# Causal-attention maxima over 64 queries of two heads instead of 128 queries of one, with the query stacks interleaved to match

## The chip, the cores and the metric

The kernel runs on one core of a Trainium2 chip. The metric is the device time of one execution in microseconds, from the first to the last instruction with the little that lies around them. Five engines work beside each other: TensorE (PE, with its weight loads PEld), VectorE (DVE), ScalarE (ACT), GpSimd (POOL) and SyncE (SP), which here only issues transfers.

## The reference

A pre-norm transformer layer on x of shape (4, 512, 1024), in float32: attention with 32 heads of 32, one shared key and value head (multi-query), ALiBi biases and a causal mask, and then a linear layer with 6-bit weights that are unpacked from int32.

```python
x = x + attn(layernorm(x), Wq, Wkv, Wo)
x = x + ffn(layernorm(x), qweight, weight_scale, weight_zero_point, bias)

def attn(hidden, Wq, Wkv, Wo):
    q = (hidden @ Wq).reshape(b, s, 32, 32)
    kv = hidden @ Wkv
    k, v = kv[..., :32], kv[..., 32:]
    scores = einsum('bqhd,bkd->bhqk', q, k) * 32 ** -0.5
    scores = where(causal, scores + slopes[:, None, None] * (pos_k - pos_q), -inf)
    attn = softmax(scores, axis=-1)
    return einsum('bhqk,bkd->bqhd', attn, v).reshape(b, s, h) @ Wo

def ffn(x, qweight, weight_scale, weight_zero_point, bias):
    w = (unpack_6_bit(qweight) - weight_zero_point) * weight_scale
    return einsum('bsk,nk->bsn', x, w) + bias
```

## The kernel before

Every float32 operand of a large matmul is split into a high part of few bits and the rest, both float32r, and the products hi*hi, hi*lo and lo*hi are summed in PSUM. `split` (lines 412 and 415) does this: ScalarE copies (`qh`, `aT`, `xT`, `xc`), VectorE subtracts (`ql` and the like).

Attention goes in 32 steps `i = b * 8 + g`, one for each batch element b and group g of four heads (`GH`). A step has three parts, which overlap with those of the steps around it:

- `queries` (products `pq`, L682): 24 products of 512 columns give the 128 rows of the group's queries (4 heads x 32) over 512 tokens in one PSUM buffer (`ps_q`, one). `qh` and `ql` go to HBM (`q_d`) and come back as a stack `qs` of 126 rows: 32 rows of qh, 32 of ql, 32 of qh again, 28 rows of biases (`qr_d`, prepared by the host), and two rows for the maxima. All these transfers have line 420. The stack has the layout (row, head, token); three are held.
- `maxima` (products `s`, L739): for each head and each tile t of 128 queries, the stack's 124 rows of these queries are the weights, and the keys `kst` up to the tile's end, 128(t+1) columns, stream past. The results go to PSUM buffers of 512 columns (`ps_s`, two), in banks that `S_BANKS` lists: 11 a step, 512 | 512 | 512 | 512 | 384 | 384 | 384 | 384 | 256+256 | 256+256 | 128 x 4. VectorE adds a causal mask and takes the maximum of each query over its keys (`junk`, L752). The maxima `mx` (128 x 16) are turned by TensorE (`trm`, L768), split (`mt0` by ScalarE, L774, and `mt1` by VectorE, L779), and written by two small transfers into the last two rows of the stack.
- `attention` (products `st`, L820): the keys are the weights and the stack streams, so that the scores come transposed (keys on partitions), with bias and minus the maximum already in. ScalarE takes the exponential (`p`, L830). For each of four key tiles GpSimd zeroes the upper triangle of the diagonal block of all four heads in one select (L839). TensorE multiplies by the values (`pav`, L849), GpSimd adds the four key tiles' p (L861), and TensorE sums them over the keys (`den`, L878). ScalarE copies pav to `a` (L867), which goes to `at_d` in HBM. `invert` takes the reciprocals of a batch element's denominators (L890).

After that come 16 token tiles: the output projection (`po`, L1048), the second layer norm, the linear layer (`pf`, L1168).

The order on each engine isn't written by hand. Every operation is recorded in `Work` with a cost, its inputs and its outputs; `order` then lists all of them by a model of the five engines and the transfers, several times forward and backward, and the instructions are issued in the order that came out. All ordinary transfers of the stacks go through one SP queue, in that order too. So a change in the cost or number of a few operations can move others on every engine.

Of the kernel before, what the change touches and what calls it, by code (L numbers as in the profile page):

```python
# [31 lines left out]
F32 = mybir.dt.float32  # L33
# [9 lines left out]
P = 128  # L43
NH = 32
HD = 32
GH = 4
S = 512
# [25 lines left out]
def bias_rows():  # L73
# [21 lines left out]
    qr = qr.reshape(NH // GH, GH, N_BIAS, S).transpose(0, 2, 1, 3)  # L95
# [246 lines left out]
def layer_kernel(  # L342
# [30 lines left out]
    for name, bufs in (  # L373
        ("const", 1), ("w", 2 * NG), ("xc", KC + 2), ("x", 4), ("qs", 3), ("q1", 1), ("p0", 2),
        ("pj", 1), ("stg", 3), ("kv", 2), ("small", 4), ("mt", 2),
    ):
        pool(name, bufs)
# [41 lines left out]
    def move(dst, src):  # L419
# [3 lines left out]
    qr_d = tc.dram_tile([NG, N_BIAS, GH, S], F32R, name="qr_d")  # L423
    at_d = tc.dram_tile([NG, P, B * S], F32, name="at_d")
    q_d = tc.dram_tile([4, 2, P, S], F32R, name="q_d")
# [16 lines left out]
    nc.gpsimd.affine_select(  # L442
        out=mask(),
        in_=mask(),
        pattern=[[-1, S]],
        compare_op=ALU.is_ge,
        fill=MASKED,
        base=S - P,
        channel_multiplier=1,
    )  # L450
# [14 lines left out]
    def prep_rows(at, g):  # L465
        dma(
            at, 229e3, lambda: nc.gpsimd.dma_start(out=qr_d[g], in_=q_rows[g]), [qr_i[g]], [],
            eng="POOL",
        )
# [205 lines left out]
    def queries(at, i):  # L675
# [15 lines left out]
        split(at, S, qh, ql, pq, qh, ql, pq)  # L691

        qs[i] = [(0, GH, new("qs", "qs", [P, GH, S], F32R, f"qs_{i}"))]
        for s, src in enumerate((qh, ql)):
            dma(
                at + 0.6 + 0.7 * s, 262e3,
                lambda s=s, src=src: move(q_d[i % 4, s], src()), [q_i[i % 4][s]], [src],
            )
        for h, n, q in qs[i]:
            dma(  # L700
                at + 1.0, 57e3 * n,
                lambda h=h, n=n, q=q: move(q()[R_BIAS:R_MAX, :, :], qr_d[g, :, h : h + n, :]),
                [(q, "b")], [qr_i[g]],
            )
            for r in range(3):
                dma(
                    at + 3.0 + 0.1 * r, 65e3 * n,
                    lambda r=r, h=h, n=n, q=q: move(
                        q()[ts(r, HD), :, :],
                        q_d[i % 4, r % 2, h * HD : (h + n) * HD].rearrange(  # L710
                            "(h d) q -> d h q", d=HD
                        ),
                    ),
                    [(q, r)], [q_i[i % 4][r % 2]],
                )

    def part(i, h):

        return next((q, h - first) for first, n, q in qs[i] if first <= h < first + n)


    S_BANKS = [((t, h),) for t in (3, 2) for h in range(GH)]
    S_BANKS += [tuple((1, h) for h in (2 * i, 2 * i + 1)) for i in range(2)]
    S_BANKS += [tuple((0, h) for h in range(GH))]
    ROWS = (0, 1, 2, "b")

    def maxima(at, i):
        b = i // NG
        k = kst[b % 2]
        mx = new("small", "mx", [P, GH * NT], F32, f"mx_{i}")  # L730
        for n, bank in enumerate(S_BANKS):
            ps = new("ps_s", "s", [P, S], F32, f"s_{i}_{n}")
            widths = [(t + 1) * P for t, _ in bank]
            places = [sum(widths[:m]) for m in range(len(bank))]

            def products(ps=ps, bank=bank, widths=widths, places=places):
                for (t, h), W, o in zip(bank, widths, places):
                    q, at = part(i, h)
                    nc.tensor.matmul(  # L739
                        ps()[:, o : o + W], q()[0:R_MAX, at, ts(t, P)], k()[0:R_MAX, :W],  # L740
                        start=True, stop=True,
                    )
            pe(
                at + 1.2 * n, widths, products, [ps],
                [(q, r) for q in {part(i, h)[0] for _, h in bank} for r in ROWS] + [k],
                more=sum(45.0 if w == P else 5.0 for w in widths),
            )
            for (t, h), W, o in zip(bank, widths, places):
                junk = new("q1", "junk", [P, S], F32, f"junk_{i}_{t}_{h}")
                dve(  # L750
                    at + 1.2 * n + 0.3, W,
                    lambda ps=ps, junk=junk, t=t, h=h, W=W, o=o: nc.vector.tensor_tensor_reduce(  # L752
                        out=junk()[:, :W],
                        in0=ps()[:, o : o + W],
                        in1=mask()[:, S - W :],
                        scale=1.0,
                        scalar=-3e38,
                        op0=ALU.add,
                        op1=ALU.max,
                        accum_out=mx()[:, h * NT + t : h * NT + t + 1],  # L760
                    ),
                    [(mx, (t, h))], [ps], more=125.0,
                )
        at += 1.2 * len(S_BANKS)
        N = GH * NT
        tr = new("ps_misc", "misc", [P, P], F32, f"trm_{i}")
        pe(
            at, [P], lambda: nc.tensor.transpose(tr()[0:N, :], mx(), ident()), [tr], [mx]  # L768
        )
        for s in range(2):  # L770
            m = new("mt", f"mt{s}", [N, P], F32R, f"mt{s}_{i}")
            if s == 0:
                hi = m
                act(at + 0.2, P, lambda: nc.scalar.copy(hi(), tr()[0:N, :]), [hi], [tr])  # L774
            else:
                lo = m
                dve(
                    at + 0.4, P,
                    lambda: nc.vector.tensor_tensor(  # L779
                        lo(), tr()[0:N, :], hi().bitcast(F32), ALU.subtract  # L780
# [3 lines left out]
            for h, n, q in qs[i]:  # L784
                dma(
                    at + 0.5 + 0.2 * s, 2e3 * n,
                    lambda m=m, s=s, h=h, n=n, q=q: move(
                        q()[R_MAX + s : R_MAX + s + 1, :, :], m()[h * NT : (h + n) * NT, :]
                    ),
                    [(q, f"m{s}")], [m],  # L790
                )
# [6 lines left out]
    def attention(at, i):  # L798
        b, g = divmod(i, NG)
        k = kst[b % 2]  # L800
# [5 lines left out]
        for n, (j, heads) in enumerate(ST_BANKS):  # L806
# [3 lines left out]
            runs = []  # L810
            for first, m, q in qs[i]:
                lo, hi = max(first, heads[0]), min(first + m, heads[-1] + 1)
                if lo < hi:
                    runs.append((
                        q, slice(lo - first, hi - first), slice(lo - heads[0], hi - heads[0])
                    ))

            def products(ps=ps, j=j, runs=runs):
                for q, mine, place in runs:
                    nc.tensor.matmul(  # L820
                        ps()[:, place, :], k()[0:R_ALL, ts(j, P)], q()[0:R_ALL, mine, j * P :],
                        start=True, stop=True,
                    )
            pe(
                at + 1.2 * n, [len(heads) * W / len(runs)] * len(runs), products, [ps],
                [q for q, _, _ in runs] + [k], more=5.0,
            )
# [8 lines left out]
            if done[j] == GH:  # L836
                def select(j=j):
                    d = pr[j]()[:, :, 0:P]
                    nc.gpsimd.affine_select(  # L839
                        out=d, in_=d, pattern=[[0, GH], [1, P]], compare_op=ALU.is_ge,  # L840
                        fill=0.0, base=0, channel_multiplier=-1,
                    )
                pool_op(at + 1.2 * n + 0.9, 650.0, select, [pr[j]], [pr[j]])
# [23 lines left out]
        act(at + 15.4, S, lambda: nc.scalar.copy(a(), pav()), [a], [pav])  # L867
# [433 lines left out]
```

## Time and profile before

| | |
|---|---|
| median of 3 runs | 828.51 us (828.41 to 833.47) |
| the profiled execution's own time | 830.86 us |
| its span, first to last instruction | 828.9 us |
| granted TensorE clock, mean | 0.993 |
| TensorE busy | 802.1 us |
| VectorE busy | 572.4 us |
| GpSimd busy | 515.7 us |
| ScalarE busy | 369.4 us |
| DMA share of the hardware queue | 57.4% of 16 engines |

"Busy" counts an instruction from its start to its end; TensorE's matmuls overlap, so its busy share is no measure of how much work it could still take. The chain of work that ended last is followed back from the last instruction: at each step to what released it. The first 535 us or so are attention, the rest the token tiles.

### The profile page before, as it was taken

To read this page: it belongs to the slowest core of one execution; us is meant where nothing else is said; L and a number is where in the kernel's file an instruction comes from. 1 tells how busy PE (TensorE), PEld (TensorE's weight loads), DVE (VectorE), ACT (ScalarE), POOL (GpSimd) and SP (SyncE) were. 2 spreads that over 40 slices of the span, in tenths; PEclk is the share of its full clock that TensorE was granted. 3 is DMA by queue.
4 is the path that set the end of the run, shared out by engine and by line. 5 is a ranking of instruction groups with operands and counts; after the bars stand their busy time and mean duration, and the time that the engine had idled before them with its cause. 6 is when DMAs were issued, how large, how long until landed. Compare 5 with 4: busy or idle time off the path is not lost.

```text
span 828.9 us, 13434 instructions
## 1 busy us (share of the span) xinstructions
PE 802.1 (97%) x4480; PEld 595.8 (72%) x4480; DVE 572.4 (69%) x1491; ACT 369.4 (45%) x659; POOL 515.7 (62%) x442
## 2 busy tenths in 40 slices
PE   5989999999999999999999999999999999999997
PEld 5766677776566767666766667667888888888885
DVE  7576876478676469866358656645988867678755
ACT  4336664545665354755365564340142323333320
POOL 4337968285968185876388997778556445554323
PEclk9989999999999999999999999999999999999999
DMA  7997662486742397463457774626975675565321
GB/s 221 245 249 214 186 173 63 123 221 216 207 112 82 91 257 227 116 162 113 153 138 220 200 215 141 232 51 165 254 169 137 138 184 127 137 164 131 102 51 51
DMA packets 131796, 133.39 MB, mean 161 GB/s; under 512 B 42964, under 2 KB 93140, under 8 KB 130704
## 3 DMA queue, kind: packets, MB, share of 16 engines
q1 hardware_dynamic: 130912, 129.01, 57.4%
q0 software_dynamic: 816, 3.53, 1.5%
q8 instruction: 35, 0.57, 0.3%
q14 instruction: 33, 0.27, 0.1%
HBM read 85.58 MB, written 39.85 MB: 151 GB/s over the span
## 4 chain that ended last, share of the span: by engine, by line
PE 87%; DMA 4%; DVE 4%; issue 2%; POOL 1%; ACT 1%; SPq 0%; DVEq 0%; ACTq 0%; POOLq 0%
PE po L1048 21%; PE pq L682 18%; PE pf L1168 13%; PE s L739 9%; PE st L820 9%; PE pav L849 8%; PE den L878 3%; PE pkv L616 2%; PE tr L598 2%; DVE junk L752 2%; POOL p L861 1%; DMA q_d<-ql 1%; DMA qs<-q_d 1%; ACT p L830 1%; DMA qs<-qr_d 1%
## 5 line engine op out<-in xcount | busy, mean ns | idle before, releaser
L752 DVE CUSTOM_DVE_ANT_0 junk<-s,mask 128x256 f32<-128x256 f32 (+3 forms) x512 | 250.4, 489 | 123.2 <-PE s L739 92.1
L861 POOL TENSOR_TENSOR p<-p,p 128x1536 f32<-128x1536 f32 (+2 forms) x96 | 230.4, 2400 | 20.2 <-PE pav L849 18.2
L830 ACT ACTIVATE p<-st 128x512 f32<-128x512 f32 (+1 forms) x352 | 184.0, 560 | 115.1 <-PE st L820 111.7
L682 PE MATMUL pq<-xc,wqh 128*128 128x512 f32 x512 | 195.8, 402 | 1.5 <-DVE ql L415 1.4
L1048 PE MATMUL po<-woh,aT 128*128 128x512 f32 x512 | 165.7, 390 | 0.0
L839 POOL TENSOR_SCALAR_AFFINE_SELECT p<-p 128x512 f32<-128x512 f32 x128 | 81.9, 645 | 104.4 <-ACT p L830 103.7
L739 PE MATMUL s<-kst,qs 124*128 124x256 f32 (+3 forms) x512 | 138.4, 339 | 7.0 <-DVE mx L752 3.3
L820 PE MATMUL st<-qs,kst 126*128 126x512 f32 (+1 forms) x352 | 125.6, 395 | 3.1 <-ACT p L830 2.6
L1168 PE MATMUL pf<-wf,xT 128*128 128x512 f32 x512 | 120.8, 390 | 0.7 <-DVE xT L415 0.7
L739 PEld LDWEIGHTS s<-kst,qs 124*128 124x128 f32 x512 | 89.0, 193 | 44.1 <-DVE mx L752 16.3
L682 PEld LDWEIGHTS pq<-xc,wqh 128*128 128x128 f32 x512 | 97.6, 191 | 21.6 <-DVE ql L415 2.1
L1048 PEld LDWEIGHTS po<-woh,aT 128*128 128x128 f32 x512 | 96.2, 188 | 21.4 <-ACT a L867 0.8
L1168 PEld LDWEIGHTS pf<-wf,xT 128*128 128x128 f32 x512 | 95.8, 188 | 21.5 <-DVE xT L415 1.7
L682 PE MATMUL pq<-xc,wql 128*128 128x512 f32 x256 | 101.6, 397 | 0.0
L1048 PE MATMUL po<-wol,aT 128*128 128x512 f32 x256 | 99.7, 390 | 0.0
L820 PEld LDWEIGHTS st<-qs,kst 126*128 126x128 f32 x352 | 65.0, 190 | 24.1 <-ACT p L830 9.7
L849 PE MATMUL pav<-p,kv 128*32 128x512 f32 (+3 forms) x1024 | 79.4, 436 | 0.4 <-POOL p L839 0.4
L849 PEld LDWEIGHTS pav<-p,kv 128*32 128x32 f32 x1024 | 29.9, 109 | 50.7 <-issue 38.0
L1188 POOL TENSOR_TENSOR x<-x,y 128x512 f32<-128x512 f32 x30 | 43.0, 1438 | 26.4 <-DVE y L1179 26.4
L1048 PEld LDWEIGHTS po<-wol,aT 128*128 128x128 f32 x256 | 48.1, 188 | 9.6
L1146 POOL TENSOR_TENSOR x<-x,rows 128x512 f32<-128x512 f32 x32 | 43.9, 1391 | 17.3 <-issue 10.1
L682 PEld LDWEIGHTS pq<-xc,wql 128*128 128x128 f32 x256 | 49.0, 191 | 5.8
(92 smaller groups left out, 850.5 us busy)
## 6 DMA issues: line engine op xcount, KB each, us to landing
qs<-q_d SPq DMA_DIRECT2D x96, 256.0 KB
x<-_attn_hidden_states_dram SPq DMA_DIRECT2D x31, 512.0 KB
q_d<-qh SPq DMA_DIRECT2D x32, 256.0 KB
q_d<-ql SPq DMA_DIRECT2D x32, 256.0 KB
at_d<-a SPq DMA_DIRECT2D x32, 256.0 KB
raw<-at_d SPq DMA_DIRECT2D x16, 512.0 KB
raw<-rden_d SPq DMA_DIRECT2D x64, 128.0 KB
out_dram<-x SPq DMA_DIRECT2D x32, 256.0 KB
```

Source lines behind the costliest of these rows:

```text
L682: nc.tensor.matmul(pq(), w()[:, c, :], xc[b, c]()[:, s, :], start=(c == 0 and n == 0), stop=(c == KC - 1 and n == 2),)
L739: nc.tensor.matmul(ps()[:, o : o + W], q()[0:R_MAX, at, ts(t, P)], k()[0:R_MAX, :W], start=True, stop=True,)
L752: lambda ps=ps, junk=junk, t=t, h=h, W=W, o=o: nc.vector.tensor_tensor_reduce(out=junk()[:, :W], in0=ps()[:, o : o + W], in1=mask()[:, S - ...
L820: nc.tensor.matmul(ps()[:, place, :], k()[0:R_ALL, ts(j, P)], q()[0:R_ALL, mine, j * P :], start=True, stop=True,)
L830: lambda ps=ps, own=own, j=j: nc.scalar.activation(pr[j]()[:, own, :], ps(), AF.Exp),
L839: nc.gpsimd.affine_select(out=d, in_=d, pattern=[[0, GH], [1, P]], compare_op=ALU.is_ge, fill=0.0, base=0, channel_multiplier=-1,)
L849: nc.tensor.matmul(pav()[ts(h, HD), j * P :], kv[b]()[:, j, HD:], pr[j]()[:, h, :], start=(j == 0), stop=(j == NT - 1), tile_position=(0, ...
L861: nc.gpsimd.tensor_tensor(d, d, pr[j](), ALU.add)
L1048: nc.tensor.matmul(po(), aT[s][1]()[:, c, :], w()[:, ts(n, HALF)], start=(c == 0 and m == 0), stop=(c == KC - 1 and m == 2),)
L1146: nc.gpsimd.tensor_tensor(d, d, rows["bias"][n][1](), ALU.add)
L1168: nc.tensor.matmul(pf(), xT()[:, s, c, :], wf[c]()[:, ts(n, HALF)], start=(c == 0 and s == 0), stop=(c == KC - 1 and s == 1),)
L1188: (nc.vector if last else nc.gpsimd).tensor_tensor(d, d, y(), ALU.add)
```

## The change

The maxima are taken for 64 queries of two heads at a time. With 64 queries a block ends at a multiple of 64, so the keys that stream past are 64, 128, ... 512 columns wide: 16 products a step as before, with 4,608 columns instead of 5,120. `S_BANKS` pairs them into nine banks of 512 columns: 512 | 512 | 448+64 (twice) | 384+128 (twice) | 320+192 (twice) | 256+256. For the 128 weight columns to have one step, the tokens of a tile are interleaved in the stacks: position 2m+o holds token 64o+m. So:

- `qh` and `ql` are written with a step of two words; `q_d` and the stack have the layout (row, tile, head, token), and the transfers between them move runs of 128 words (512 bytes) instead of 512 words; the host prepares the bias rows in that order.
- the weights of an `s` product are every second word of two heads' tile.
- the maxima are turned by two transposes of 8 columns each instead of one of 16, and `mt0` and `mt1` have 8 partitions of 256 elements instead of 16 of 128 (one buffer each instead of two).
- the causal select takes the two halves of a diagonal block one after the other, each 4 x 64 elements at a step of two.
- the copy to `a` and the reciprocals read at a step of two and put the tokens back in order.
- the model's extra cost of 45 ns for an `s` product of 128 columns is gone.

```diff
-    qr = qr.reshape(NH // GH, GH, N_BIAS, S).transpose(0, 2, 1, 3)
+    qr = qr.reshape(NH // GH, GH, N_BIAS, S // P, P // QB, QB).transpose(0, 2, 3, 1, 5, 4)
...
-        split(at, S, qh, ql, pq, qh, ql, pq)
+        def turns(t):
+            return lambda: t().rearrange("p (t m o) -> p t o m", t=NT, m=QB)
+        split(
+            at, S, turns(qh), turns(ql),
+            lambda: pq().rearrange("p (t o m) -> p t o m", t=NT, m=QB), qh, ql, pq,
+        )
+        q = qs[i] = new("qs", "qs", [P, NT, GH, P], F32R, f"qs_{i}")
...
-                lambda s=s, src=src: move(q_d[i % 4, s], src()), [q_i[i % 4][s]], [src],
+                lambda s=s, src=src: move(
+                    q_d[i % 4, s].rearrange("t p q -> p t q"),
+                    src().rearrange("p (t q) -> p t q", t=NT),
+                ),
...
+                lambda r=r: move(
+                    q()[ts(r, HD)].rearrange("d t h q -> d (t h) q"),
+                    q_d[i % 4, r % 2].rearrange("t (h d) q -> (t h) d q", d=HD).rearrange(
+                        "x d q -> d x q"
...
-    S_BANKS = [((t, h),) for t in (3, 2) for h in range(GH)]
-    S_BANKS += [tuple((1, h) for h in (2 * i, 2 * i + 1)) for i in range(2)]
-    S_BANKS += [tuple((0, h) for h in range(GH))]
+    NQ = S // QB
+    HP = GH // 2
+    S_BANKS = [((NQ - 1, u),) for u in range(HP)]
+    S_BANKS += [((NQ - 2 - m, u), (m, u)) for m in range(NQ // 2 - 1) for u in range(HP)]
+    S_BANKS += [tuple((NQ // 2 - 1, u) for u in range(HP))]
...
-            widths = [(t + 1) * P for t, _ in bank]
+            widths = [(e + 1) * QB for e, _ in bank]
...
-                for (t, h), W, o in zip(bank, widths, places):
-                    q, at = part(i, h)
+                for (e, u), W, at in zip(bank, widths, places):
+                    t, o = divmod(e, P // QB)
+                    rows = q()[0:R_MAX, t].rearrange("p h (m o) -> p o (h m)", m=QB)
                     nc.tensor.matmul(
-                        ps()[:, o : o + W], q()[0:R_MAX, at, ts(t, P)], k()[0:R_MAX, :W],
+                        ps()[:, at : at + W], rows[:, o, ts(u, P)], k()[0:R_MAX, :W],
                         start=True, stop=True,
                     )
...
-                more=sum(45.0 if w == P else 5.0 for w in widths),
...
-            at, [P], lambda: nc.tensor.transpose(tr()[0:N, :], mx(), ident()), [tr], [mx]
+            for o in range(P // QB):
+                nc.tensor.transpose(tr()[0:N, o, :], mx()[:, o, :], ident())
...
-                def select(j=j):
-                    d = pr[j]()[:, :, 0:P]
-                    nc.gpsimd.affine_select(
-                        out=d, in_=d, pattern=[[0, GH], [1, P]], compare_op=ALU.is_ge,
-                        fill=0.0, base=0, channel_multiplier=-1,
-                    )
-                pool_op(at + 1.2 * n + 0.9, 650.0, select, [pr[j]], [pr[j]])
+                for o in range(P // QB):
+                    def select(j=j, o=o):
+                        d = pr[j]()[:, :, 0:P].rearrange("p h (m o) -> p h m o", m=QB)[:, :, :, o]
+                        nc.gpsimd.affine_select(
+                            out=d, in_=d, pattern=[[0, GH], [1, QB]], compare_op=ALU.is_ge,
+                            fill=0.0, base=o * QB, channel_multiplier=-1,
+                        )
+                    pool_op(at + 1.2 * n + 0.9, 400.0, select, [pr[j]], [pr[j]])
...
-        act(at + 15.4, S, lambda: nc.scalar.copy(a(), pav()), [a], [pav])
+        act(
+            at + 15.4, S,
+            lambda: nc.scalar.copy(
+                a().rearrange("p (t o m) -> p t o m", t=NT, m=QB),
+                pav().rearrange("p (t m o) -> p t o m", t=NT, m=QB),
+            ),
+            [a], [pav],
+        )
```

## Prediction, made before the result was known

> **What bounds the kernel now.** I read first the busy times and the chain of work that ended last, then groups by shape, then single stretches.
>
> ```profile
> PE 802.1 (97%) x4480; PEld 595.8 (72%) x4480; DVE 572.4 (69%) x1491; ACT 369.4 (45%) x659; POOL 515.7 (62%) x442
> ...
> PE 87%; DMA 4%; DVE 4%; issue 2%; POOL 1%; ACT 1%; SPq 0%; DVEq 0%; ACTq 0%; POOLq 0%
> ```
>
> The chain runs through TensorE for 87% of 828.9 us. So a nanosecond taken from TensorE's own work counts in full, and one taken from another engine counts only where TensorE stands waiting for it. The places where it does are few. The chain of waits shows them:
>
> ```profile
> 32.50 7.62 DMA q_d<-ql
> 40.14 7.60 DMA qs<-q_d
> ...
> 443.45 3.47 POOL p L861
> ```
>
> At the start the second group's queries go out to HBM and come back as a stack, 7.6 us each way, with nothing else to do; near 443 us GpSimd's adds are late. The share by line adds 1.6% for `DVE junk L752`, that is 13.3 us of VectorE's maxima, scattered over the attention steps. Next, what one product of the maxima costs:
>
> ```profile
> 366.37 0.40 PE L739 MATMUL s<-kst,qs 124*128 124x256 f32 x2
> 366.61 0.39 PE L820 MATMUL st<-qs,kst 126*128 126x512 f32 x1
> ...
> 368.01 0.56 PE L739 MATMUL s<-kst,qs 124*128 124x128 f32 x4
> 368.41 0.62 PE L820 MATMUL st<-qs,kst 126*128 126x512 f32 x2
> ...
> 369.56 0.40 PE L739 MATMUL s<-kst,qs 124*128 124x512 f32 x1
> 369.79 0.34 PE L820 MATMUL st<-qs,kst 126*128 126x384 f32 x1
> 369.97 0.40 PE L682 MATMUL pq<-xc,wqh 128*128 128x512 f32 x1
> ```
>
> First number: start. The pitch (start to next start) is what counts, since durations overlap: 512 columns 0.23 us, 384 columns 0.18, 256 columns 0.24/2 = 0.12, 128 columns 0.40/4 = 0.10. From 512 to 256 the pitch falls with the columns; 128 would then cost 0.055 but takes 0.10. Narrow products have a floor.
>
> **The change, part by part** (32 steps, one for each group of four heads of a batch element).
>
> *Products of the maxima.* Before, 4 heads x widths 128, 256, 384, 512: 4 x (0.10 + 0.12 + 0.18 + 0.23) = 2.52 us a step. After, 2 pairs x widths 64 to 512 in steps of 64; between rows I interpolate: 0.11 for 192, 0.15 for 320, 0.205 for 448, and the floor for 64: 2 x (0.10 + 0.10 + 0.11 + 0.12 + 0.15 + 0.18 + 0.205 + 0.23) = 2.39. That is -0.13 x 32 = -4.2 us. Unknown: the 64-wide product, between 0.03 (columns alone, another -4.5 us) and 0.10; I take 0.10, the pitch of the nearest row, 128. Unknown too: the weights, which are now every second word of a stack row. No row has such a load. At worst each narrow product costs the duration of a load, 0.193 us (rival 1); a gain is excluded, since no load gets fewer words. I take no change.
>
> *One transpose more.* The maxima are turned by two matmuls instead of one:
>
> ```profile
> 329.83 0.11 PE trm L768
> ```
>
> 0.11 x 32 = +3.5 us, on TensorE. The copy to mt0 takes 256 elements for 128 (0.247 us; by ScalarE's 0.586 at 512, 0.36), the subtraction to mt1 0.423 (the row of kv<-trkv,part, 256 elements) for 0.273: together 0.26 us later for the two rows that end the stack. In the new order at least 4.2 us of TensorE work stands between trm and the first st product (4.1 before), so these are hidden; uncovered they would cost 0.26 x 32 = 8 us.
>
> *VectorE's maxima.*
>
> ```profile
> L752 DVE CUSTOM_DVE_ANT_0 junk<-s,mask 128x512 f32<-128x512 f32 x128 | 88.2, 689 | 51.2 <-PE s L739 42.6 <-DVE mx L752 0.5
> ...
> L752 DVE CUSTOM_DVE_ANT_0 junk<-s,mask 128x128 f32<-128x128 f32 x128 | 37.2, 291 | 9.8 <-PE s L739 3.3
> ```
>
> (689 - 291)/384 = 1.036 ns an element, plus 158 and an 83 ns read of the accumulator. The mean width falls from 320 to 288: 33 ns x 512 = 17 us less of VectorE. Only waits of TensorE give time back. I counted, in the order of both built programs with every matmul at its pitch, the places where a product needs one of the two PSUM buffers before VectorE can have read it: 18 places, 8.9 us before; 13 places, 3.1 us after (nine full banks a step instead of eleven). Against that trm now stands closer behind the last products (3.6 us in the mean, from 5.7): 1.4 us of new waiting. Sum -4.4; ends -13.3 (all of the chain's share) and 0.
>
> *The causal select by halves.*
>
> ```profile
> 1.07 0.29 POOL masks.py:199 TENSOR_SCALAR_AFFINE_SELECT ident<-ident 128x128 f32<-128x128 f32 x1
> ...
> 1.94 0.61 POOL L442 TENSOR_SCALAR_AFFINE_SELECT mask<-mask 128x512 f32<-128x512 f32 x1
> ```
>
> 0.83 ns an element and 0.18 fixed: 256 elements take 0.40. Two for one of 0.645 is +0.155, x 128 = +20 us of GpSimd. Mostly idle time takes it (GpSimd waits 104 us for p at that line), but not everywhere:
>
> ```profile
> 450.00:500.00 50.00, 48.94 (x301) 33.16 (x300) 33.35 (x124) 31.61 (x64) 48.03 (x35) 1.00 0.73 208
> ```
>
> The fifth engine number is GpSimd: 48.03 of 50 us busy. Some 3.3 steps of 0.62 us fall there: +2 us. Ends: 0, and 4 if 440 to 540 us is all tight.
>
> *Stacks in 512-byte pieces.* The five 256 KB moves of a step (qh and ql out, three in) have runs of 128 words instead of 512.
>
> ```profile
> 14.00:16.00 2.00, 1.91 (x10) 1.67 (x9) 1.42 (x3) 1.59 (x4) 0.00 (x0) 1.00 0.92 247
> 16.00:18.00 2.00, 2.00 (x10) 1.59 (x10) 2.00 (x4) 2.00 (x5) 0.00 (x0) 1.00 0.88 251
> 18.00:20.00 2.00, 2.00 (x10) 1.67 (x9) 2.00 (x5) 1.52 (x4) 0.98 (x1) 1.00 0.41 121
> 22.00:24.00 2.00, 2.00 (x11) 1.65 (x10) 1.89 (x2) 0.79 (x2) 1.48 (x2) 1.00 0.35 131
> ```
>
> The last two columns are the busy share of the DMA engines and GB/s. From 22 to 24 only qh moves, in 2 KB runs: 0.35 x 2 = 0.70 us for 262 KB. From 14 to 20 it is mostly Wq, in 512-byte runs: 2.21 x 2 = 4.42 us for 1,238 KB, 0.94 us for 262 KB. So +0.24 a move, +1.2 us of DMA a step. The issue costs the queue nothing more: raw<-at_d, 512-byte runs too, takes 0.43 us there, qs<-q_d 0.42. Outside full stretches it is hidden behind queries of later steps; if it is not, see rival 2. From 26 to 58 us the DMA share is about 1.0 and the chain goes through it; 3.5 steps are +4 us of DMA work, and the new order puts about 2 us less TensorE work before the second group's products. I take +3; ends 0 and 6. The Trainium skill, "DMA: Bandwidth & Descriptors", section "Why small descriptors are slow", gives a fixed cost of about three cycles a descriptor; estimated from it, 512-byte pieces cost (16 + 3) x 4 = 76 cycles for 67, 13%, and a step +0.46 us. The row says 34%, though of a load with other runs beside it; I go by the row.
>
> *Every second word elsewhere.* qh and ql are written at step two, a and the reciprocals read at step two. VectorE's nearest row is L920, 256 lone words at steps of three and four: 0.398 us median, no more than 0.423 for the 256 above. So ql stays at 0.687; the upper end is twice that, 22 us of VectorE, mostly in idle time. ql frees the one pq buffer: by the order, the next pq stands too close behind (under 1.5 us) for 1.8 us before and 3.2 after, +1.4; with ql at twice its time +5. The Trainium skill, "Vector Engine (DVE) Microarchitecture Reference", section 5.2, speaks against this part: a stream runs at full rate only in pairs of adjacent words, about 1.75 ns a column otherwise; estimated by it ql is 0.36 us longer and that term about 3 instead of 1.4. The row doesn't show the penalty.
>
> *Sum:* -4.2 + 3.5 - 4.4 + 2 + 3 + 1.4 = +1.3 us on the profiled execution, whose own time is 830.86 us (span 828.9, 1.96 around it). The median of the runs is 828.5, 2.35 lower; so 829.8 is forecast. The order differs in many places from the old one, which I allow +-8 us: 821 to 838 for this case. A measurement of this kernel tells about 1%, 8.3 us, from no change.
>
> **Rivals.**
> 1. *Slower: weights at step two load slowly.* Place: line 739, where narrow products follow each other. If the six of each pair up to 384 wide take 0.193, a step is 2 x (6 x 0.193 + 0.205 + 0.23) = 3.19 for 2.39, +25 us: 855. Banks now pair a wide with a narrow product, and often stand beside 0.23 us ones which cover a load, so half: 842. It decides from a pitch of about 0.15 (+9 us). For: no strided load in the trace. Against: the floor of 0.10 is already under the recorded 0.193, so loads have slack.
> 2. *Slower: the queries come back late.* Path of a step: qh 0.59, ql 0.69, issue 0.34, store 0.94, three loads 2.8, and about 2.6 us landing twice (k_rows, 60 KB, lands in 2.8): 10.9 us, 9.9 before. TensorE work between the last pq and the first s: at least 10.1 (six under 11.5), before 9.4 (three under 10.8). A queue of 3 us in front (two 512 KB moves) makes the shortfalls 25 us instead of 15: +10, so 840. For: stretches of share 1.0. Against: the chain meets this path only at the start.
> 3. *Faster: the waits for maxima all go,* and selects and moves are hidden: -4.2 + 3.5 - 13.3 + 1.4 = -12.6, so 816. For: nine even banks. Against: VectorE keeps 94% of its work here.
>
> **How the numbers follow.** Forecast 0.40, rival 1 0.15, rival 2 0.18, rival 3 0.27. Leaving a tenth out on either side: 813 to 846. The forecast's tails past 1% are small; faster 0.28, same 0.39, slower 0.33.
>
> **What would show it.** Right: pitch 0.10 at 64 and 128 columns, trm 0.11 twice, selects near 0.40, the junk group near 230 us busy for 250, its share of the chain near 1%. Wrong: a pitch over 0.15 at line 739 (rival 1); qs<-q_d in the chain after 100 us (rival 2); `DVE junk` nearly gone from the chain (rival 3); selects above 0.5, which would add 13 us and more to GpSimd's full stretch and the steps around it.

## The result, and the profile after

The changed kernel takes 840.82 us (median of 4 runs, 837.96 to 842.78); the kernel before, beside it, 829.46 (median of 4). The ratio is 1.0129, 95% interval 1.010 to 1.0157: slower by a little over one per cent. 829.8 was forecast, 813 to 846 as the range, 821 to 838 for the forecast's own case.

The profiled execution takes 841.85 us (span 840.1, 828.9 before; mean granted clock 0.988). From its page, first the busy times and the chain of work that ended last:

```profile
PE 799.9 (95%) x4512; PEld 598.7 (71%) x4512; DVE 552.5 (66%) x1491; ACT 374.0 (45%) x659; POOL 540.7 (64%) x571
...
PE 78%; DMA 8%; DVE 5%; POOL 3%; ACT 2%; issue 2%; SPq 1%; DVEq 0%; POOLq 0%; ACTq 0%
```

TensorE is busy 2.2 us less in a span 11.2 us longer, and VectorE 19.9 us less. The chain has lost nine points to other engines: DMA from 4 to 8%, GpSimd from 1 to 3%. From the same page the two groups whose price was forecast (busy, mean ns of one | idle before, and what ended it) and the hardware DMA queue (packets, MB, share of 16 engines), first before, then after:

```profile
q1 hardware_dynamic: 130912, 129.01, 57.4%
...
L752 DVE CUSTOM_DVE_ANT_0 junk<-s,mask 128x256 f32<-128x256 f32 (+3 forms) x512 | 250.4, 489 | 123.2 <-PE s L739 92.1
...
L839 POOL TENSOR_SCALAR_AFFINE_SELECT p<-p 128x512 f32<-128x512 f32 x128 | 81.9, 645 | 104.4 <-ACT p L830 103.7
```

```profile
q1 hardware_dynamic: 191328, 129.01, 61.4%
...
L762 DVE CUSTOM_DVE_ANT_0 junk<-s,mask 128x448 f32<-128x448 f32 (+7 forms) x512 | 233.5, 456 | 130.1 <-PE s L749 102.8
...
L847 POOL TENSOR_SCALAR_AFFINE_SELECT p<-p 128x256 f32<-128x256 f32 x256 | 106.3, 440 | 96.5 <-ACT p L837 95.7
```

The maxima take 233.5 us (about 230 forecast), a half select 0.440 us (0.40). The queue's time is 61.4% of 840.1 for 57.4% of 828.9: 40.0 us more on all 16 engines, over 160 moves of 256 KB 0.25 us each (0.24 forecast; the layout alone, in `pieces` below, gives 34.8 us, 0.22 each). Of the operations at step two only qh became slower, from 587 to 630 ns: ql takes 690 (687 before), the copy to a 587 (590), the reciprocals 919 (934). Estimated from the 1.75 ns a column of the Trainium skill, "Vector Engine (DVE) Microarchitecture Reference", section 5.2, ql would be some 0.36 us longer; these rows do not show it. mt0 takes 369 ns in the median and mt1 408 (0.36 and 0.423 forecast).

Next the products of the maxima. The timeline of TensorE (start, duration, what, how many) in the changed kernel, around 362 us:

```profile
362.05 0.40 PE L749 MATMUL s<-kst,qs 124*128 124x448 f32 x2
362.29 0.42 PE L829 MATMUL st<-qs,kst 126*128 126x384 f32 x1
362.55 0.40 PE L749 MATMUL s<-kst,qs 124*128 124x448 f32 x2
362.78 0.47 PE L686 MATMUL pq<-xc,wqh 128*128 128x512 f32 x1
363.10 0.40 PE L686 MATMUL pq<-xc,wql 128*128 128x512 f32 x1
363.33 0.39 PE L686 MATMUL pq<-xc,wqh 128*128 128x512 f32 x1
```

The two products 448 + 64 (named by the first form) take 0.24 us together, as if the 64 columns cost only their columns. But the product behind them takes 0.32 us to the next start (362.78 to 363.10), where the one after it takes 0.23 (363.10 to 363.33). The floor of a narrow product is there; it is paid at the next start. Over all such places from 100 to 550 us, the median of the following 512-column product is 0.31 behind 448 + 64, 0.28 behind 384 + 128, 0.25 behind 320 + 192 and 0.23 behind 256 + 256. So 64, 128 and 192 columns all cost about 0.11 us. (In the kernel before, the product behind four of 128 takes 0.29.)

**Where TensorE's time went.** From each product's start to the next one's, put down to the earlier, with recorded idle time put down to the product that waited, in the two profiled executions (us):

| | before | after | difference |
|---|---|---|---|
| s | 102.4 | 84.9 | -17.5 |
| trm | 2.0 | 9.5 | +7.5 |
| st | 90.1 | 95.4 | +5.3 |
| pq | 185.4 | 195.1 | +9.7 |
| po | 175.1 | 180.1 | +5.0 |
| pav and den | 105.1 | 105.6 | +0.5 |
| pf | 117.6 | 117.6 | 0.0 |

The maxima's products give 17.5 us. All of it and 10 more goes to others: part is the price of narrow products paid by the next one, part the second transpose, the rest waits and products at a lower clock. Two places stand out.

*The start.* The same timeline near 50 us, with the idle time before a product in brackets:

```profile
48.61 0.79 PE L686 MATMUL pq<-xc,wqh 128*128 128x512 f32 x1 [4.30 <-ACT wqh L491]
49.98 0.79 PE L686 MATMUL pq<-xc,wql 128*128 128x512 f32 x1 [0.57 <-POOL wql L493]
50.57 1.05 PE L686 MATMUL pq<-xc,wqh 128*128 128x512 f32 x2
51.42 0.63 PE L686 MATMUL pq<-xc,wql 128*128 128x512 f32 x1
```

and single stretches of it (busy time of PE, PEld, DVE, ACT, POOL; granted clock; busy share of the DMA engines; GB/s):

```profile
42.00:46.00 4.00, 1.01 (x4) 0.43 (x4) 3.74 (x12) 0.38 (x1) 1.18 (x1) 0.86 1.18 232
46.00:50.00 4.00, 0.82 (x2) 0.31 (x2) 1.02 (x5) 3.00 (x4) 2.34 (x4) 0.50 1.16 271
50.00:54.00 4.00, 4.00 (x10) 3.13 (x11) 0.00 (x0) 0.83 (x2) 1.66 (x2) 0.50 0.75 243
```

TensorE waits 4.3 us for a piece of Wq, whose transfer now stands behind the weights of the linear layer and the first stacks in SP's queue, while the DMA engines are full. The granted clock is 0.50 from about 45 to 55 us, so through most of the wait and some 6.5 us behind it, and a product of 512 columns takes 0.43 us instead of 0.23 (50.57 to 51.42 is two). The kernel before has such a stretch too, from about 53 us on, behind shorter waits. From 30 to 60 us TensorE is busy 21.83 us, before 25.67.

*The handover to the token tiles.* The last `st` starts at 555.59 us, before at 556.45: attention as a whole seems no slower. But before it 26 `pf` products had been done in the old order and 4 in the new one, and 16 `pav` products that stood before it now stand behind it: 22 x 0.23 + 1.6 = 6.7 us of work was left for later. The next tile's `po` waits for `raw` (the attention output times the reciprocals, on GpSimd), and `raw` for its transfers. From this tile on they use the buffers of p, so they can be issued only when `den` of the step before the last has read one, and `den` stands behind GpSimd's adds. The timeline of the kernel before (SPq is an issue):

```profile
543.43 1.29 POOL L861 TENSOR_TENSOR p<-p,p 128x512 f32<-128x512 f32 x1
...
546.18 0.38 SPq L1008 DMA_DIRECT2D raw<-at_d  x1
...
548.74 1.71 PE L849 MATMUL pav<-p,kv 128*32 128x512 f32 x16
550.38 6.23 PE L1168 MATMUL pf<-wf,xT 128*128 128x512 f32 x26
550.69 3.51 POOL L861 TENSOR_TENSOR p<-p,p 128x1536 f32<-128x1536 f32 x1
554.16 2.40 POOL L1025 TENSOR_TENSOR raw<-raw 128x1024 f32<-128x1024 f32 x1
556.45 0.40 PE L820 MATMUL st<-qs,kst 126*128 126x512 f32 x1
556.68 5.17 PE L1168 MATMUL pf<-wf,xT 128*128 128x512 f32 x22
...
561.69 0.39 PE L1048 MATMUL po<-woh,aT 128*128 128x512 f32 x1
```

and of the changed one:

```profile
544.90 3.76 POOL L869 TENSOR_TENSOR p<-p,p 128x1024 f32<-128x1024 f32 x2
...
551.02 0.38 SPq L1026 DMA_DIRECT2D raw<-at_d  x1
...
555.59 0.40 PE L829 MATMUL st<-qs,kst 126*128 126x512 f32 x1
555.92 1.71 PE L857 MATMUL pav<-p,kv 128*32 128x512 f32 x16
...
557.52 3.50 POOL L869 TENSOR_TENSOR p<-p,p 128x1536 f32<-128x1536 f32 x1
557.56 11.18 PE L1186 MATMUL pf<-wf,xT 128*128 128x512 f32 x48
560.97 2.40 POOL L1043 TENSOR_TENSOR raw<-raw 128x1024 f32<-128x1024 f32 x1
...
568.58 0.39 PE L1066 MATMUL po<-woh,aT 128*128 128x512 f32 x1
...
586.81 0.47 PE L1066 MATMUL po<-woh,aT 128*128 128x512 f32 x1 [2.82 <-DVE x L1076]
```

The adds of the step before the last end at 548.66 us for 544.72, the issue is 4.8 us later, the last step's long add stands ahead of `raw` in both, and `po` goes on 6.9 us later. TensorE does not stand idle for that: the work left over fills the time. It pays one tile later. The next tile's transfers can start only when `aT` has read the late `raw` (issue at 566.10, before 561.27), its `raw` ends at 577.4, and behind the additions that follow TensorE waits 2.82 us for `x`, before the `po` at 586.81; the kernel before has no recorded wait of `po`. The granted clock then falls to 0.50 for some 3.5 us, which makes the `po` products about 1.5 us slower in all.

From the start of the last `st` to the end of the last `po` it is 262.5 us, before 251.2. With the 6.7 us taken off, the token tiles lose 11.3 - 6.7 = 4.6 us, and attention, which left them that work, -0.9 + 6.7 = 5.8. Together 10.4, nearly all of the loss of this profile (11.0).

In the chain of waits (start, us, what), seven transfers of the stacks now stand between 60 and 560 us, 37.6 us together. In the kernel before there were two, 10.6 us together:

```profile
220.91 5.02 DMA qs<-mt
351.44 5.57 DMA qs<-qr_d
```

In the changed one these are among them:

```profile
101.88 5.46 DMA qs<-q_d
184.74 5.29 DMA qs<-qr_d
257.22 5.80 DMA qs<-qr_d
338.72 5.57 DMA qs<-mt
```

### The profile page after: what moved, and what is told of

Same layout as the page of the kernel before. It is cut to its first block, busy times and chain, and to the rows that moved or that the text cites. A ratio compares the mean times of both kernels' runs of the same rounds, so it can differ in the third digit from the quotient of the medians.

```text
span 840.1 us, 13606 instructions
## 1 busy us (share of the span) xinstructions
PE 799.9 (95%) x4512; PEld 598.7 (71%) x4512; DVE 552.5 (66%) x1491; ACT 374.0 (45%) x659; POOL 540.7 (64%) x571
## 3 DMA queue, kind: packets, MB, share of 16 engines
q1 hardware_dynamic: 191328, 129.01, 61.4%
## 4 chain that ended last, share of the span: by engine, by line
PE 78%; DMA 8%; DVE 5%; POOL 3%; ACT 2%; issue 2%; SPq 1%; DVEq 0%; POOLq 0%; ACTq 0%
PE po L1066 20%; PE pq L686 17%; PE pf L1186 12%; PE st L829 8%; PE s L749 7%; PE pav L857 7%; PE den L893 3%; DMA qs<-qr_d 3%; PE pkv L620 2%; PE tr L602 2%; DMA wo_st<-in_L_attn_Wo_dram 1%; POOL p L869 1%; DVE junk L762 1%; DMA qs<-mt 1%; ACT p L837 1%
## 5 line engine op out<-in xcount | busy, mean ns | idle before, releaser
L762 DVE CUSTOM_DVE_ANT_0 junk<-s,mask 128x448 f32<-128x448 f32 (+7 forms) x512 | 233.5, 456 | 130.1 <-PE s L749 102.8
L686 PE MATMUL pq<-xc,wqh 128*128 128x512 f32 x512 | 200.4, 408 | 6.2 <-ACT wqh L491 4.3
L847 POOL TENSOR_SCALAR_AFFINE_SELECT p<-p 128x256 f32<-128x256 f32 x256 | 106.3, 440 | 96.5 <-ACT p L837 95.7
L829 PE MATMUL st<-qs,kst 126*128 126x512 f32 (+1 forms) x352 | 129.0, 405 | 6.7 <-ACT p L837 4.1
L749 PE MATMUL s<-kst,qs 124*128 124x448 f32 (+7 forms) x512 | 116.9, 312 | 4.0 <-DMA qs<-qr_d 2.1
L749 PEld LDWEIGHTS s<-kst,qs 124*128 124x128 f32 x512 | 94.4, 198 | 29.5 <-issue 9.3
L1164 POOL TENSOR_TENSOR x<-x,rows 128x512 f32<-128x512 f32 x32 | 46.6, 1472 | 11.1 <-DVE x L1087 6.4
```

The lines of the kernel that those rows point to most:

```text
L686: nc.tensor.matmul(pq(), w()[:, c, :], xc[b, c]()[:, s, :], start=(c == 0 and n == 0), stop=(c == KC - 1 and n == 2),)
L749: nc.tensor.matmul(ps()[:, at : at + W], rows[:, o, ts(u, P)], k()[0:R_MAX, :W], start=True, stop=True,)
L762: nc.vector.tensor_tensor_reduce(out=junk()[:, :W], in0=ps()[:, place : place + W], in1=mask()[:, S - W :], scale=1.0, scalar=-3e38, op0=A ...
L829: nc.tensor.matmul(ps().rearrange("p h (t q) -> p h t q", q=P), k()[0:R_ALL, ts(j, P)], q()[0:R_ALL, j:, own].rearrange("p t h q -> p h t q"),
L847: nc.gpsimd.affine_select(out=d, in_=d, pattern=[[0, GH], [1, QB]], compare_op=ALU.is_ge, fill=0.0, base=o * QB, channel_multiplier=-1,)
L1164: nc.gpsimd.tensor_tensor(d, d, rows["bias"][n][1](), ALU.add)
```

## The experiments

Three theories were on trial. D: the moves in 512-byte runs bring queries and stacks back late. P: the second select holds GpSimd up. O: the planner's new order of the same work, not any price, makes the loss. Every experiment was timed against the kernel before on its own chip (medians 827.8 to 828.4 us).

**The 512-byte layout alone** (`pieces`): the kernel before with the order (row, tile, head, token) in the stacks and in HBM. The order on every engine stays that of before.

```diff
-    q_d = tc.dram_tile([4, 2, P, S], F32R, name="q_d")
+    q_d = tc.dram_tile([4, 2, NT, P, P], F32R, name="q_d")
-        qs[i] = [(0, GH, new("qs", "qs", [P, GH, S], F32R, f"qs_{i}"))]
+        qs[i] = [(0, GH, new("qs", "qs", [P, NT, GH, P], F32R, f"qs_{i}"))]
```

> The kernel before, with only the layout of the stacks and of the queries in HBM changed to (row, tile, head, token), so that the five 256 KB moves of a step go in runs of 512 bytes; tokens are not interleaved, the products, the selects and the order on every engine are those of before. Theory D (the 512-byte moves bring the queries back late, and this is most of what the change loses): 836 us or more, with waits for the stack in the chain after 100 us. Theory O (the new order loses most, and its own prices little): the moves cost what they cost at the start, +2 to +5 us, 831 to 834. Theory P (the second select on GpSimd): no change, 829.

835.34 us, ratio 1.009 (1.0065 to 1.0115): 7 us, between what D (836 or more) and O (831 to 834) expected. Its chain, by engine:

```profile
PE 85%; DMA 6%; DVE 3%; ACT 2%; issue 1%; POOL 1%; SPq 1%; DVEq 0%; ACTq 0%; POOLq 0%
```

DMA goes from 4 to 6%, with nothing else changed. So D has a price of its own, over twice the 3 us of the forecast. In this profile the last `st` is 4.0 us later than before and the stretch from there to the end of `po` is 251.2 us, to the tenth that of before: the price falls in attention alone, spread over it (TensorE busy 438.55 us from 100 to 550 us, before 442.17), not at the start, where the forecast had put it. How the longer moves reach TensorE is shown only in part: its recorded waits for stacks rise from 1.7 to 2.8 us, those for the maxima by 0.7, those for the exponentials by 0.5, and 2.0 us more have no releaser in the profile.

**The second select alone** (`selects2`): each select of before as two halves inside one recorded operation, again in before's order.

```diff
-                    d = pr[j]()[:, :, 0:P]
-                    nc.gpsimd.affine_select(
-                        out=d, in_=d, pattern=[[0, GH], [1, P]], compare_op=ALU.is_ge,
+                    for o in range(2):
+                        d = pr[j]()[:, :, ts(o, P // 2)]
+                        nc.gpsimd.affine_select(
+                            out=d, in_=d, pattern=[[0, GH], [1, P // 2]], compare_op=ALU.is_ge,
```

> The kernel before, with each causal select done as two, of the two halves of the diagonal block, in the same place of the same order (the model of the planner is told of one operation of 650 ns). Some 0.2 us more of GpSimd for each of 128 blocks, +24 us busy. Theory P: +6 us or more, 835. Theories D and O: 0 to +3 us, since GpSimd idles over 100 us in front of this line; 829 to 832.

832.52 us, ratio 1.006 (1.003 to 1.0089): 4 us, for 19 us more of GpSimd (534.6 busy; the halves are of adjacent words here and take 429 ns each, 440 in the changed kernel). That lies between P (835) and the others (829 to 832). P too has a price, twice the 2 us of the forecast, but a loosely known one: the ten runs go from 828.69 to 838.34. Where it falls is not shown, since the profiled run is the fastest of the ten, with a span 2.1 us under that of before's profile; in it GpSimd's share of the chain goes from 1 to 3%:

```profile
PE 89%; DVE 3%; POOL 3%; issue 1%; ACT 1%; DMA 1%; SPq 0%; DVEq 0%; ACTq 0%; POOLq 0%
```

**Both together** (`both`), still in before's order:

> The kernel before, with the 512-byte layout of the stacks and with each causal select as two halves in one recorded operation; the order on every engine is that of before. Alone the two cost 7 and 4 us. If they are prices of their own (theories D and P together, each on its own stretch of the chain): 10 to 12 us over before, ratio 1.013, which is the whole of the change's loss, so that the order would have nothing left to explain except what the cheaper products gave back. If they lean on the same slack (a stack that comes late gives GpSimd time): 7 to 8 us, 1.009.

836.44 us, ratio 1.0106 (1.0086 to 1.0126): 8.2 us, less than 7 + 4. The two may lean partly on the same slack, but the interval reaches from the one expectation to the other. Its chain:

```profile
PE 78%; DMA 8%; DVE 4%; POOL 4%; issue 3%; ACT 2%; SPq 1%; DVEq 0%; POOLq 0%; ACTq 0%
```

It is nearly the chain of the changed kernel. But the place differs: here the last `st` is 8.5 us late and the token tiles again take their 251.2; in the changed kernel, where TensorE has cheaper products, attention loses 5.8 us and the tiles 4.6.

**The same work in other orders** (`shaken`, `shaken2`): the kernel before, instruction for instruction, with one figure of the planner's model changed.

```diff
-                more=sum(45.0 if w == P else 5.0 for w in widths),
+                more=0.0,
```

> The kernel before with the same instructions in another order: the planner's model is not told of the 45 ns extra for a product of 128 columns (as in the changed kernel). It measures what an order alone moves. Theory O: a difference of 5 us or more, of either sign, with the same busy times; D and P: under 3 us.

```diff
-DMA_RATE = 280.0
+DMA_RATE = 270.0
```

> The kernel before with the same instructions in a second other order: the planner's model has a DMA rate of 270 instead of 280. Theory O: 833 to 842, like the first shaken one (836.9), which would make the order of before a good one among its like; if it is within 3 us of 828.4, an order moves less than that run said.

836.86 us, ratio 1.0094 (1.0065 to 1.0123), and 833.65, ratio 1.0063 (1.0043 to 1.0083). An order alone moves this kernel by 5 to 8 us, and both of these moved it up: of the three orders tried the one that the kernel before has is the fastest. In the first, the stretch from the last `st` to the end of `po` is 257.5 us instead of 251.2, with 4.2 us of recorded waits of `po` for `x`: the same place, and the same wait, as in the changed kernel, without any of its moves or selects.

**The planner told of the prices** (`told`): the changed kernel, in which the model counts the 256 KB moves and the selects as they are.

```diff
-                at + 0.6 + 0.7 * s, 262e3,
+                at + 0.6 + 0.7 * s, 350e3,
...
-                at + 3.0 + 0.1 * r, 262e3,
+                at + 3.0 + 0.1 * r, 350e3,
...
-                    pool_op(at + 1.2 * n + 0.9, 400.0, select, [pr[j]], [pr[j]])
+                    pool_op(at + 1.2 * n + 0.9, 430.0, select, [pr[j]], [pr[j]])
```

> The changed kernel, with the planner's model told that a 256 KB move in 512-byte runs costs 350 instead of 262 (in its units of kB) and a half select 430 ns instead of 400. The same instructions in another order. Theory D: the planner now leaves room for the moves, 828 to 836 instead of 841. Theory O: it lands anywhere from 828 to 845, and the waits sit in other places. Theory P: no change, 839 to 842.

830.84 us, ratio 1.0033 (1.0019 to 1.0047): the same work, the same moves, 8 us less than the changed kernel by the two ratios (10 by the medians, which are of different chips) and 0.3% over before. The timeline at the handover:

```profile
547.16 0.38 SPq L1026 DMA_DIRECT2D raw<-at_d  x1
...
554.67 2.40 POOL L1043 TENSOR_TENSOR raw<-raw 128x1024 f32<-128x1024 f32 x1 [0.51 <-DMA raw<-rden_d]
557.03 3.51 POOL L869 TENSOR_TENSOR p<-p,p 128x1536 f32<-128x1536 f32 x1
...
565.22 0.39 PE L1066 MATMUL po<-woh,aT 128*128 128x512 f32 x1
```

The transfers are issued 3.9 us earlier than in the changed kernel, and `raw` is now ahead of the long add: it waits 0.51 us for its own transfer and for nothing else. The wait of `po` for `x` is 0.2 us instead of 2.8, and the 4.3 us wait for Wq at the start is gone from the waits. Of the 9.1 us between the two spans, with work left over counted where it belongs, 3.4 come back in attention, 4.3 at the handover and 1.5 at the end. So most of the loss can be given back without touching a move or a select, which refutes P as the whole cause. The time fits D's expectation (828 to 836) as well as O's; but a later order, `unturn270` below, is told of the moves' price too and takes 838.5, so being told is not what does it.

**One select for the two halves** (`one_select`: the changed kernel; `told_one`: the kernel told of the prices). The pattern walks half by half inside each pair of positions, so its innermost run is 2.

```diff
-                for o in range(P // QB):
-                    def select(j=j, o=o):
-                        d = pr[j]()[:, :, 0:P].rearrange("p h (m o) -> p h m o", m=QB)[:, :, :, o]
...
+                def select(j=j):
+                    d = pr[j]()[:, :, 0:P].rearrange("p h (m o) -> p h m o", m=QB)
...
+                        out=d, in_=d, pattern=[[0, GH], [1, QB], [QB, P // QB]],
```

> The changed kernel with one causal select for each diagonal block and nothing told. Theory P: 840.8 - 5 = 836. Theory D: the moves keep it above 836, waits for the stack stay in the chain. Theory O: the order is new again, 828 to 845, without connection to GpSimd's busy time.

> The changed kernel with the planner told of the moves' cost (350 for 262) and with one causal select for each diagonal block, of 512 contiguous elements, whose pattern holds the interleave (64 m + 2 o steps in one instruction). 24 us less of GpSimd. Theory P (the second select is worth the 0.6% that it cost at the old order): 826 us, 4 to 6 below the 830.8 of the run that was only told. Theory O (orders differ by 1%): anywhere from 822 to 838. Theory D: 830.

971.38 us, ratio 1.1733 (1.1709 to 1.1757), and 971.05, ratio 1.1729 (1.1708 to 1.1749): a miss. The group in `one_select`:

```profile
L846 POOL TENSOR_SCALAR_AFFINE_SELECT p<-p 128x512 f32<-128x512 f32 x128 | 298.4, 2344 | 59.1 <-ACT p L837 59.1
```

2.34 us for 512 elements, where runs of 128 take 0.645. GpSimd becomes the bound, and the two orders come out alike. On theory P this tells only that enough GpSimd time is fatal.

**The linear layer's weights a step later** (`late`, on top of `told_one`):

```diff
-        unpack(T0 + (1.6 + 2.0 * (c % 3) + NG * (c // 3)) * STEP, c)
+        unpack(T0 + (2.6 + 2.0 * (c % 3) + NG * (c // 3)) * STEP, c)
```

> As the kernel that was told and has one select, and the unpacking of the first weight block (a 384 KB load, a transpose and a 512 KB store) starts one step of 15 us later, so that the stretch from 26 to 60 us with full DMA engines holds less. Theory D: the start gains back the 4 to 6 us of TensorE that the changed kernel lost from 30 to 100 us: 820 to 826. Theory O: no connection; 822 to 838.

981.28 us, ratio 1.1852 (1.1827 to 1.1877). With GpSimd as the bound it says nothing of the start; it was tried again below on a sound base.

**The halves put back by the exponential** (`unturn`): the kernel told of the prices, in which ScalarE's exponential reads its scores at a step of two and writes p in token order. The select is again one instruction in runs of 128, and the copy to a and the reciprocals are plain.

```diff
-                    pr[j]()[:, own, :], ps(), AF.Exp
+                    pr[j]()[:, own, :].rearrange("p h (t o m) -> p (h t) o m", o=P // QB, m=QB),
+                    ps().rearrange("p h (t m o) -> p (h t) o m", o=P // QB, m=QB), AF.Exp,
```

> The changed kernel with the planner told of the moves' price (350e3 for 262e3), in which the exponential reads its PSUM buffer at a step of two and writes p in token order: the causal select is again one instruction of 4 x 128 in runs of 128, and the copy to a and the reciprocals are plain. Theory P: the selects go back from 106 to 82 us, and about 4 us of the chain come back against the 830.8 us of the kernel that only tells the planner: 826 to 828, ratio 0.997 to 1.000. If the exponentials at step two cost (their mean of 512 columns over 0.62 us), ScalarE is later by the excess x 288. Theory O: a new order moves it by up to 6 us either way whatever the selects do.

830.79 us, ratio 1.0027 (1.0016 to 1.0039). From its page, the chain and the groups of the exponential and the select:

```profile
PE 90%; DVE 4%; issue 2%; ACT 1%; DMA 1%; POOL 0%; SPq 0%; DVEq 0%; ACTq 0%
...
L837 ACT ACTIVATE p<-st 128x512 f32<-128x512 f32 (+1 forms) x352 | 183.8, 559 | 118.7 <-PE st L829 111.6
...
L847 POOL TENSOR_SCALAR_AFFINE_SELECT p<-p 128x512 f32<-128x512 f32 x128 | 81.5, 643 | 117.0 <-ACT p L837 116.6
```

The step of two costs the exponential nothing (559 ns with and without), and the selects are back at 81.5 us. GpSimd has left the chain, from 6% in `told` to nothing; DMA went from 6 to 1%. The chain of `told`:

```profile
PE 80%; POOL 6%; DMA 6%; DVE 3%; issue 2%; ACT 2%; SPq 1%; POOLq 0%; DVEq 0%
```

The time stayed. The 826 to 828 us of theory P is missed: the 4 us of the second select that before's order had shown are not to be had here, or the new order took them. A chain share is not a price; what left the chain was replaced by waits for VectorE (`s` behind the maxima 5.2 us, in `told` 3.2) and by TensorE itself.

**The same with the later unpacking** (`unturn_late`: the edit of `late`) **and in another order** (`unturn270`: the edit of `shaken2`):

> The same, with the unpacking of the feed-forward weights recorded one step (15 us) later, so that its reads and writes of HBM leave the stretch from 26 to 58 us, in which the transfers are full. Theory D (the start is lost to the transfers' extra 0.25 us each): TensorE's busy time from 30 to 60 us rises from the 22.7 us of the told kernel to 24.5 or more, and the time falls by 2 to 4 us against the same kernel with the early unpacking: 823 to 826. If not the load of the transfers but the round trip of the first two groups' queries holds the start: no change there, and the time within 2 us.

> The kernel with the exponential in token order, the planner's DMA rate 270 for 280: the same instructions in another order. Theory O: 2 to 8 us from the same kernel at 280, either way, as two other orders of the kernel before were 5.5 and 8 us from it. If the order matters little in the changed kernel (nine even banks lean less on it): within 2 us.

`unturn_late`: 830.31 us, ratio 1.0037 (1.0018 to 1.0056). TensorE's busy time from 30 to 60 us rises from 24.13 us in `unturn` to 25.30; the 22.7 that the expectation started from is of `told`. The time expected, 2 to 4 us less, did not come: the medians differ by 0.5 us. The profiled execution, the fastest of its runs, shows where: its last `st` starts 5.1 us earlier than in `unturn`, but from 550 to 600 us TensorE is busy 47.65 us instead of 50.00, with a 2.3 us wait of `po` for `x`, and its span is only 1.8 us shorter. So a late start alone does not set the end.

`unturn270`: 838.5 us, ratio 1.0119 (1.0101 to 1.0137): 8 us from its twin by an order alone, so the changed kernel leans on its order as much as the kernel before.

No version beat the kernel before. The best of the changed ones stand 0.3 to 0.4% above it.

## Why the prediction was right and wrong

The time fell in the range, but 3 us past the forecast's own case. Slower by over 1% had been given 0.33, the forecast's side 0.39: the likeliest case did not come, and no single rival did either. That the range held is owed to its width and not to the sum, which said +1.3 us where 11 came; that rival 2 named 840 is luck, as shown below. Term by term, forecast against what the runs show:

- *Products, -4.2: right.* Own pitches after: 2 x 0.23 + 6 x 0.235 + 0.24 = 2.11 us a step, and 2 x (0.08 + 0.05 + 0.025) = 0.31 at the next starts, 2.42; before 2.52 and 0.06, 2.58. That is -0.16 x 32 = -5.1. The floor of 0.10 was the right guess, though it is paid one product later. Rival 1 is refuted: the loads at step two take 198 ns in the mean, 193 before, and no place shows a pitch that they could have made.
- *VectorE's waits, -5.8: the sign was right, the size is open.* Of the 17.5 us that `s` gave, (2.52 - 2.11) x 32 = 13.1 is own pitch, which leaves 4.4 for waits. Recorded are 2.8 (6.7 before, 3.9 after), and of these 1.7 for the maxima (3.3 and 1.6). Rival 3 is refuted: junk keeps about 1% of the chain.
- *Second transpose and trm's waits, +3.5 + 1.4: short.* trm costs 7.5 us more, of which 2.7 are recorded waits (for `xc` 1.4 and for the maxima 1.3). The 0.11 was one place; in the mean a trm before took 0.06 to the next start, 2.0 us in all. The later rows of maxima were put at nothing, as hidden: recorded waits of `st` for them rose from 0.3 to 2.4 us.
- *Moves, +3: mis-sized, 7 measured alone.* The price of a move was right (0.25 us for 0.24, 36% of 0.70). The 13% estimated from the Trainium skill's page "DMA: Bandwidth & Descriptors", section "Why small descriptors are slow", is not what the runs show. Wrong was the cover: the forecast charged only the full stretch at the start (+3 there) and let queries of later steps hide the rest; alone, the layout cost nothing at the start and all of its price in those later steps. Rival 2 had this mechanism, and its sign came, though barely: `qs<-q_d` stands once in the chain after 100 us, at 101.88. But it put the whole loss down to it; with cheaper products beside it, recorded waits of TensorE for stacks rose only from 1.7 to 4.7 us. (The pieces that it lists for its path add to 10.6 and 9.6 us, not 10.9 and 9.9; the difference of 1 us stands.)
- *Selects, +2: mis-sized, 4 measured alone* (429 ns each there, 440 in the changed kernel, 400 forecast), with an interval from 2.5 to 7.4. The forecast charged one full stretch of GpSimd. Together with the moves it is 8.2, forecast 5.
- *pq buffer, +1.4: not seen.* Recorded waits of `pq` for `ql` are 1.4 us before and 1.2 after.
- *The order, 0 with +-8: this is where the rest is.* The new order costs 4.6 us at the handover, where GpSimd's last adds and with them `raw` came late; `told`, with the same instructions, pays 0.3 there. It was allowed for as a spread around zero. Two other orders of the kernel before and one of `unturn` cost 5 to 8 us, and no order of either kernel gave less than before's; that an order so good was likely to lose when redrawn could not be known without such runs.

With these sizes the sum is -5.1 + 7.5 - 4.4 + 8.2 + 4.6 = +10.8 for 11.0 us between the two profiles, and without the handover +6.2 for the 5.8 that attention loses. It mixes several runs, so its last 1 or 2 us mean nothing. Nor are its terms prices that hold in any order: the 8.2 of moves and selects was measured in before's order, and `told`, which has the same moves and selects, is only 2 to 3 us over before. What stays open: how the longer moves reach TensorE; how far the second select costs anything outside before's order (`unturn` says no, `selects2` yes), and which part of the changed kernel's loss in attention the wait for Wq at the start makes, since taking the load off that stretch moved the time elsewhere.

## What to carry to other kernels

Where a planner draws the order anew, an edit has two prices: its own, which can be measured by making it inside one recorded operation so that the order stays, and that of the new order, which here was as large; redraw the old kernel's order a few times first to learn how large. And look at the seams between phases: the time from the last instruction of one phase to the end of the next, less the work that the first phase left over, tells which phase lost. A share of the chain is a place to look, not a price: DMA and GpSimd fell from 12% of it to 1% with no gain in time.

## What the runs showed of the hardware

- GpSimd's select, for 512 elements: 0.645 us in runs of 128; as two instructions of 256 in runs of 64, 2 x 0.429 of adjacent words (`selects2`) and 2 x 0.440 at a step of two; 2.34 with an innermost count of 2 (`one_select`).
- A product of 64 to 192 columns beside a wide one takes its columns' time, and the next product pays 0.02 to 0.08 us; in all some 0.11, as four of 128 in a row.
- Float32 at a step of two cost little: ScalarE's copy 587 ns (590), its exponential of 512 columns 598 (598), VectorE's subtraction 690 (687) and reciprocal 919 (934), TensorE's weight load 198 (193). The one that shows a price is ScalarE's `qh`, which writes at that step: 630 ns (587), and 627 to 640 in `told` and the three `unturn` kernels.
- A 256 KB move in runs of 512 bytes instead of 2 KB took 0.22 to 0.25 us more of all 16 DMA engines, on 0.70.
- Around a wait of 4.3 us the granted clock was 0.50 for about 10 us, 6.5 of them behind the wait, and a 512-column product took 0.43 us instead of 0.23; after a wait of 2.82 us it was 0.50 for about 3.5 us.
